# New places in the engines' orders for the Mamba tiles of a four-layer convolution network

## The chip, the cores and the metric

The kernel runs on one core of one Trainium2 chip. The time is that of one execution on the device in microseconds (us); less is better. Three runs of the kernel before gave 7575.1, 7577.68 and 7587.97 us, median 7577.68. A further execution was taken by the profiler: 7595.04 us, with a span of 7593.2 us between its first and last instruction.

## What is computed

The input x is (2, 128, 128, 128) in float32: two images, 128 channels, 128 rows, 128 columns. Four layers follow each other. Layers 0 and 2 are Mamba layers, each with its own weights; layer 1 is a density gate over windows of 8 x 8; layer 3 is a residual block of two 3x3 convolutions with signs as weights. The change touches the Mamba layers alone. At every pixel the 128 channels of a 3x3 convolution are read as a sequence of 8 tokens of 16 features:

```python
seq = conv3x3(x).reshape(B * H * W, 8, 16)
xi, z = split(seq @ in_proj_w.T)                    # 32 each
xc = silu(causal_conv1d(xi) + conv1d_b)
dt, Bm, Cm = split(xc @ x_proj_w.T)                 # 1, 16, 16
dt = softplus(dt @ dt_proj_w.T + dt_proj_b)
dA, dBx = exp(dt * A), dt * Bm * xc                 # 32 x 16 states
h = dA * h + dBx;  y = sum(h * Cm)                  # token after token
out = ((y + D * xc) * silu(z)) @ out_proj_w.T       # 8 x 16 = 128 channels
x = x + silu(group_norm(out))
```

The scan over 8 tokens with 32 x 16 = 512 states a pixel is most of the work.

## The kernel before

A tile (`k` in the code) is 4 image rows, 512 pixels. There are 32 tiles an image, 64 a Mamba layer, 128 in all. All of this is `_mamba` (line 289 on); line numbers are those of the profile.

The work of one tile. `band` loads 8 rows with a border, for two tiles (L191). `conv` is nine matmuls on TensorE (L323) and a copy by ScalarE; `turn` transposes four blocks (L339) and copies; `project` makes xc and z (L350, copies L352 and L354), `silu` L357. `step` makes dt (L364, L365), `softplus` L368. `inout` makes B and C (L400, copy L407), `product` their product on GpSimd (L412), `own` the share of each token's own input (L420, copy L421); `scaled` is u = dt * xc on GpSimd (L374), `own_u` two GpSimd operations (L425, L427) with a scaling by ScalarE between them (L426). `store` writes u and B, C to DRAM in ten small DMAs (L382, L389); `load` reads them back for one token, replicated over the state partitions, in four DMAs: `ur` (L435, L436) and `bcr` (L439, L440). `inject` multiplies the two on GpSimd (L445, 128x2048). `decay` is eight small matmuls (L454) and two exponentials (L463), one for each half of the states; `token` does, for each half, the product with the old state (L472), with C (L473) and the sum of the new state (L477, not for the last token) on VectorE. `gather` sums over the states (L492), onto what `through` put into the same bank (L483); `gate` multiplies with z (L505), `out` is the last matmul (L512, copy L520), `spread` the statistics (L523), `keep` the DMA to y (L527).

Buffers that matter: three `ur`, five `bcr`, four `h`; three PSUM buffers for the decays, of which every decay takes two; one PSUM bank ("one") for all small products and the convolution; one bank ("ys") for the sums and the output. Token 7 of a tile is its last, and token 1 of the next tile comes right behind it; token 0 is the inject of token 0.

The order of every engine is written out by hand. Each step has a place in tokens, relative to its tile's start; a tile is SPAN = 7 tokens long. All steps of all tiles are sorted by `k * SPAN + place` and issued in that order, and each engine works through its own part of the list strictly in order, as data and buffers permit. Thus in the steady state the places of three to four tiles interleave: while tile k is scanned, k+1 is stored and loaded, k+2 is convolved and projected. The first tiles of a layer have an order of their own (`early`), which the change leaves. `token` has fixed places: token t, half jp, at t - 1 + jp / 2. All places are constants:

```python
put(k, REP_AT + t, decay, t)
put(k, t - 1 + jp / 2, token, t, jp)
put(k, SUM_AT + t, gather, t)
```

In the built instruction stream the DMAs of SP carry eight completion semaphores in turn: each waits until the one eight before it has landed, beside its own data and buffers.

Of the kernel before, what the change touches and what calls it, by code (L numbers as in the profile page):

```python
# [266 lines left out]

SPAN = NT - 1
BAND_AT = -22.0
CONV_AT = (-12.75, -12.7, -11.6, -11.5, -11.35, -11.25, -11.2, -11.05, -10.85)  # L270
TURN_AT = -10.5
IN_AT = (-10.0, -9.75, -9.65, -9.05)
SILU_AT = -8.52
BC_AT = (-8.25, -7.45)
DT_AT = (-7.85, -6.7)
SOFTPLUS_AT = -5.62
PROD_AT = -6.85
OWN_AT = (-6.3, -5.8)
U_AT, OWN_U_AT = -5.0, -4.3
STORE_AT = -4.15  # L280
LOAD_AT, INJECT_AT = -3.7, -1.8
REP_AT = -1.2
SUM_AT = 0.35
D_AT = (1.25, 4.2)
V_AT = (3.79, 7.39)
OUT_AT, STATS_AT, KEEP_AT = 7.9, 12.5, 13.85


def _mamba(tc, src, w, con, dst, scratch, stats, H):
# [264 lines left out]
    def put(k, at, f, *args):  # L554
        at = early.get((k, f, *args), k * SPAN + at)
        todo.append((at, len(todo), f, (k, *args)))


    for k in range(len(src) * ntile):
        if k * ROWS % BAND == 0:  # L560
            put(k, BAND_AT, band)
        for tap in range(9):
            put(k, CONV_AT[tap], conv, tap)
        put(k, TURN_AT, turn)
        for n in range(4):
            put(k, IN_AT[n], project, *divmod(n, 2))
        for name in ("xc", "zs"):
            put(k, SILU_AT, silu, name)
        for i in range(2):
            put(k, BC_AT[i], inout, i)  # L570
        for g in range(2):
            put(k, DT_AT[g], step, g)
        put(k, SOFTPLUS_AT, softplus)
        put(k, PROD_AT, product)
        put(k, U_AT, scaled)
        for g in range(2):
            put(k, OWN_AT[g], own, g)
        put(k, OWN_U_AT, own_u)
        put(k, STORE_AT, store)
        for t in range(NT - 1):  # L580
            put(k, LOAD_AT + t, load, t)
            put(k, INJECT_AT + t, inject, t)
        for t in range(1, NT):
            put(k, REP_AT + t, decay, t)
            for jp in range(2):
                put(k, t - 1 + jp / 2, token, t, jp)
            put(k, SUM_AT + t, gather, t)
        for g in range(2):
            put(k, D_AT[g], through, g)
            put(k, V_AT[g], gate, g)  # L590
        put(k, OUT_AT, out)
# [509 lines left out]
```

## Time and profile before

| | |
|---|---|
| median of 3 runs | 7577.68 us (7575.1 to 7587.97) |
| profiled execution | 7595.04 us, span 7593.2 us |
| first Mamba layer, first L472 of tile 0 to that of tile 63 | 68.4 to 3261.2 us |
| second Mamba layer | 3656.9 to 6863.9 us |
| L445 on GpSimd (inject) | 896 times, 4059.2 us, 4537 ns each |
| L472, L473, L477 on VectorE (token) | 1792, 1792, 1536 times, 1223, 1225 and 1214 ns each |
| L463 on ScalarE (exponential of decay) | 1792 times, 1007 ns each |
| DMA issued for `ur` and `bcr` | 896 each, 896 and 448 KB, 11.6 and 11.8 us to landing |
| DMA, mean over the span | 233 GB/s; 250 GB/s in the Mamba layers |

The page gives each engine's busy time, then the span in 40 slices with a digit for the tenths that an engine was busy, then groups of instructions by line with mean durations. The waits say who stood idle for whom: us in total, how often, the longest. A wait for several semaphores is put down to the one that came last. In the timeline each row is a run of equal instructions on one engine, with the idle time before it and what ended it. SPq is the queue from which SP issues DMAs.

### The profile page before, as it was taken

The page shows a single profiled execution, that of the slowest core. Times are in us where ns is not written, and L with a number is a line of the kernel's source. Part 1 is how long each engine was busy: PE and PEld are TensorE (multiplying, and loading weights), DVE is VectorE, ACT ScalarE, POOL GpSimd, SP SyncE. Part 2 cuts the span into 40 slices and gives each one's busy share as a digit, 9 for nine tenths or more (in the row PEclk, how much of TensorE's full clock was granted, in tenths as well). Part 3 has the DMA queues.
Part 4 walks back from the last instruction along what each step waited for, and adds up shares of the span by engine and source line. Part 5 has one row for each costly group of instructions (what it writes and reads, how often), then busy time and mean ns, then how long its engine had stood idle before and what let it go on. Part 6 is the DMA issues. An engine that isn't in the chain of part 4 may idle for free.

```text
span 7593.2 us, 89536 instructions
## 1 busy us (share of the span) xinstructions
PE 6291.6 (83%) x30416; PEld 2339.8 (31%) x30416; DVE 7026.3 (93%) x7082; ACT 4279.0 (56%) x4877; POOL 5538.6 (73%) x1815
## 2 busy tenths in 40 slices
PE   7888888888888888867888888888888888887994
PEld 2222222222222222234222222222222222224773
DVE  6999999999999999968699999999999999998986
ACT  5566656666656666545566656665666566562222
POOL 5778777877787788743687787878777877785641
PEclk8999999999999999977899999999999999997997
DMA  7999999999999999954899999999999999996604
GB/s 207 247 248 250 252 245 251 252 253 249 247 252 255 248 250 253 251 183 173 211 256 245 248 244 248 251 253 246 248 252 248 251 248 246 247 256 184 194 7 172
DMA packets 573737, 1769.79 MB, mean 233 GB/s; under 512 B 85568, under 2 KB 239712, under 8 KB 458208
## 3 DMA queue, kind: packets, MB, share of 16 engines
q1 hardware_dynamic: 568672, 1747.28, 88.1%
q10 hardware_dynamic: 4608, 16.78, 0.6%
q8 instruction: 242, 3.96, 0.2%
q14 instruction: 215, 1.76, 0.1%
HBM read 1552.83 MB, written 210.89 MB: 232 GB/s over the span
## 4 chain that ended last, share of the span: by engine, by line
DVE 39%; DMA 30%; PE 14%; issue 6%; POOL 5%; ACT 4%; SPq 2%; POOLq 0%; DVEq 0%; ACTq 0%
DMA bcr<-sb 23%; DVE set L472 12%; DVE h L477 10%; DVE r L473 10%; DMA ur<-su 4%; PE m L910 4%; POOL h L445 3%; PE set L454 2%; PE one L350 2%; ACT set L463 2%; PE ys L492 1%; PE ys L483 1%; DVE v L505 1%; PE one L400 1%; DVE comb L901 1%
## 5 line engine op out<-in xcount | busy, mean ns | idle before, releaser
L445 POOL TENSOR_TENSOR h<-ur,bcr 128x2048 f32<-128x2048 f32 x896 | 4059.2, 4537 | 1331.9 <-DMA bcr<-sb 1098.7
L472 DVE TENSOR_TENSOR set<-set,h 128x1024 f32<-128x1024 f32 x1792 | 2192.5, 1223 | 257.4 <-ACT set L463 153.8
L473 DVE TENSOR_TENSOR r<-set,bcr 128x1024 f32<-128x1024 f32 x1792 | 2194.4, 1225 | 61.4
L463 ACT ACTIVATE set<-set 128x1024 f32<-128x1024 f32 x1792 | 1743.7, 1007 | 790.0 <-PE set L454 776.4
L477 DVE TENSOR_TENSOR h<-set,h 128x1024 f32<-128x1024 f32 x1536 | 1865.4, 1214 | 43.7 <-POOL h L445 43.1
L454 PE MATMUL set<-dt,rep 32*128 32x512 f32 x7168 | 1385.9, 676 | 97.8 <-DVE h L477 93.5
L492 PE MATMUL ys<-r,ct 128*32 128x512 f32 x7168 | 1160.1, 634 | 33.0 <-DVE r L473 32.6
L323 PE MATMUL one<-band,conv 128*128 128x512 f32 x2304 | 1083.5, 606 | 22.6 <-DMA band<-in_x_dram 12.3
L400 PE MATMUL one<-xc,keep 128*64 128x512 f32 x1008 | 314.8, 707 | 470.3 <-ACT xc L357 355.8
L454 PEld LDWEIGHTS set<-dt,rep 32*128 32x128 f32 x7168 | 403.1, 193 | 977.0 <-issue 478.0
L323 PEld LDWEIGHTS one<-band,conv 128*128 128x128 f32 x2304 | 407.7, 190 | 669.1 <-issue 597.1
L910 PE MATMUL m<-comb,u 128*128 128x256 f32 x2304 | 510.2, 382 | 63.0 <-DVE comb L903 45.3
L483 PE MATMUL ys<-t,ct 128*128 128x512 f32 x512 | 324.5, 720 | 252.1 <-DVE v L505 250.5
L910 PEld LDWEIGHTS m<-comb,u 128*128 128x128 f32 x2304 | 437.5, 191 | 135.4 <-issue 72.0
L492 PEld LDWEIGHTS ys<-r,ct 128*32 128x32 f32 x7168 | 181.2, 111 | 911.3 <-issue 756.9
L352 ACT ACTIVATE xc<-one,keep 128x512 f32<-128x512 f32 x252 | 173.3, 688 | 509.7 <-PE one L350 504.8
L420 PE MATMUL one<-prod,ct 128*128 128x512 f32 x504 | 284.7, 648 | 148.4 <-POOL prod L412 126.7
L374 POOL TENSOR_TENSOR u<-dt,xc 128x1024 f32<-128x1024 f32 x128 | 302.6, 2364 | 78.1 <-ACT dt L368 77.8
L350 PE MATMUL one<-y,w_in 128*128 128x512 f32 x504 | 340.7, 765 | 1.7 <-ACT xc L352 1.7
L421 ACT COPY t<-one 128x512 f32<-128x512 f32 x252 | 147.7, 586 | 326.9 <-PE one L420 326.9
L463 ACT ACT_TABLE_LOAD x254 | 325.9, 1283 | 4.5
L427 POOL TENSOR_TENSOR t<-t,xc 128x1024 f32<-128x1024 f32 x128 | 302.1, 2360 | 10.0
(166 smaller groups left out, 6116.2 us busy)
## 6 DMA issues: line engine op xcount, KB each, us to landing
ur<-su SPq DMA_DIRECT2D x896, 896.0 KB, 11.6
bcr<-sb SPq DMA_DIRECT2D x896, 448.0 KB, 11.8
ur<-su SPq DMA_DIRECT2D x896, 128.0 KB, 11.2
su<-u SPq DMA_DIRECT2D x1024, 64.0 KB, 3.2
sb<-bc SPq DMA_DIRECT2D x256, 224.0 KB, 2.7
bcr<-sb SPq DMA_DIRECT2D x896, 64.0 KB, 11.1
y<-o SPq DMA_DIRECT2D x128, 256.0 KB, 9.2
band<-in_x_dram SPq DMA_DIRECT2D x28, 640.0 KB, 11.0
```

The source lines that it names most:

```text
L323: nc.tensor.matmul(py.rearrange("p (r w) -> p r w", r=ROWS), lhsT=w["conv"][:, tap, :], rhs=xb[:, r + kh : r + kh + ROWS, kw : kw + P], st ...
L350: nc.tensor.matmul(p, lhsT=w[("in", "z")[i]][:, g, :], rhs=s["y"], start=True, stop=True)
L400: nc.tensor.matmul(p[g * NQ * DS : (g + 1) * NQ * DS, :], lhsT=w[("xb", "xcm")[i]], rhs=s["xc"][:, g, :], start=True, stop=True,)
L445: nc.gpsimd.tensor_tensor(b, s["ur", t], s["bc", t][:, 0].unsqueeze(1).to_broadcast([P, NJ, NS]), ALU.mult)
L454: nc.tensor.matmul(a[j // 2][:, j % 2, :], lhsT=w["rep"][r, q, :], rhs=s["dt"][r, g, :], start=True, stop=True, tile_position=(r.start, 0),)
L463: nc.scalar.activation(x, x, AF.Exp)
L472: nc.vector.tensor_tensor(pt, pt, s["h", t - 1][:, js, :], ALU.mult)
L473: nc.vector.tensor_tensor(s["r", t][:, js, :], pt, s["bc", t - 1][:, 1].unsqueeze(1).to_broadcast([P, 2, NS]), ALU.mult)
L477: nc.vector.tensor_tensor(s["h", t][:, js, :], pt, s["h", t][:, js, :], ALU.add)
L483: nc.tensor.matmul(s["ys", g], lhsT=con["ident"], rhs=s["t1"][:, g, :], start=True, stop=False)
L492: nc.tensor.matmul(s["ys", g][a : a + NQ * DJ, :], lhsT=red[:, q, :], rhs=r[:, j, :], start=False, stop=(q == NQ - 1), tile_position=(0, a),)
L910: nc.tensor.matmul(m[:, n // 2, n % 2], lhsT=u[:, i, kw, :], rhs=v[:, i, :, kw : kw + P], start=(kw == 0), stop=(kw == 2),)
```

## The change

Only the table of places is changed. No instruction is added or taken away, no buffer changes its size, and no operation its engine.

```diff
 BAND_AT = -22.0
-CONV_AT = (-12.75, -12.7, -11.6, -11.5, -11.35, -11.25, -11.2, -11.05, -10.85)
-TURN_AT = -10.5
-IN_AT = (-10.0, -9.75, -9.65, -9.05)
-SILU_AT = -8.52
-BC_AT = (-8.25, -7.45)
-DT_AT = (-7.85, -6.7)
-SOFTPLUS_AT = -5.62
-PROD_AT = -6.85
-OWN_AT = (-6.3, -5.8)
-U_AT, OWN_U_AT = -5.0, -4.3
-STORE_AT = -4.15
-LOAD_AT, INJECT_AT = -3.7, -1.8
-REP_AT = -1.2
-SUM_AT = 0.35
-D_AT = (1.25, 4.2)
-V_AT = (3.79, 7.39)
-OUT_AT, STATS_AT, KEEP_AT = 7.9, 12.5, 13.85
+CONV_AT = (-13.2, -12.65, -12.35, -12.1, -11.8, -11.35, -11.3, -11.25, -11.0)
+TURN_AT = -10.9
+IN_AT = (-10.75, -9.2, -10.2, -9.35)
+SILU_AT = -8.87
+BC_AT = (-8.45, -8.05)
+DT_AT = (-8.0, -7.1)
+SOFTPLUS_AT = -6.02
+PROD_AT = -7.75
+OWN_AT = (-7.1, -6.5)
+U_AT, OWN_U_AT = -5.4, -3.15
+STORE_AT = -5.2
+LOAD_AT, INJECT_AT = -4.3, -1.55
+REP_AT = -1.25
+SUM_AT = 0.0
+D_AT = (0.95, 3.85)
+V_AT = (3.29, 7.44)
+OUT_AT, STATS_AT, KEEP_AT = 7.8, 8.0, 12.3
```

Only the order within one engine counts. Over one period (token 1 of tile k to token 1 of tile k+1; +1 and +2 mark steps of the tiles ahead, -1 of the tile behind) the orders become, before and after:

```
VectorE before  1.0 gate1(-1) 1.1 2.0 2.1 3.0 3.1 4.0 4.1 gate0 5.0 5.1 6.0 stats(-1) 6.1 7.0 7.1
VectorE after   1.0 gate1(-1) 1.1 stats(-1) 2.0 2.1 3.0 3.1 4.0 gate0 4.1 5.0 5.1 6.0 6.1 7.0 7.1
GpSimd before   product(+1) inject2 inject3 scaled(+1) inject4 own_u(+1) inject5 inject6 inject0(+1) inject1(+1)
GpSimd after    inject2 inject3 scaled(+1) inject4 inject5 own_u(+1) inject6 inject0(+1) product(+2) inject1(+1)
SP before       load4 load5 load6 store(+1) load0(+1) load1(+1) load2(+1) band(+4) load3(+1) keep(-1)
SP after        load5 load6 store(+1) load0(+1) load1(+1) load2(+1) keep(-1) load3(+1) band(+4) load4(+1)
TensorE before  step1(+1) gather7(-1) own0(+1) decay2 out(-1) own1(+1) through0 conv0 conv1 gather1 decay3
                gather2 conv2-5 decay4 conv6-8 gather3 turn decay5 project00 through1 project01 gather4 project10
                decay6 project11 gather5 inout0 decay7 step0 gather6 inout1 decay1(+1)
TensorE after   gather7(-1) own1(+1) decay2 out(-1) conv0 through0 gather1 conv1 conv2 decay3
                conv3 gather2 conv4-6 decay4 conv7 gather3 conv8 turn project00 decay5 project10 through1 gather4
                project11 decay6 project01 gather5 inout0 decay7 inout1 gather6 step0 decay1(+1) step1 own0
```

(project, conv, turn, inout and step without a mark belong to tile k+2, in the last row step1 and own0 too. ScalarE follows TensorE's order with its copies and exponentials; its SiLUs stay between the exponentials of tokens 6 and 7, its softplus between those of 2 and 3, and the scaling of own_u goes from before the exponentials of token 4 to behind those of token 5.)

## The prediction

> **What bounds the kernel now.** I read the page's first two parts, then who waited for whom on VectorE, then the waits of the stretch 300 to 3300 us (first Mamba layer, all tiles alike), then the timeline of single tiles.
>
> ```profile
> PE 6291.6 (83%) x30416; PEld 2339.8 (31%) x30416; DVE 7026.3 (93%) x7082; ACT 4279.0 (56%) x4877; POOL 5538.6 (73%) x1815
> ...
> DMA  7999999999999999954899999999999999996604
> GB/s 207 247 248 250 252 245 251 252 253 249 247 252 255 248 250 253 251 183 173 211 256 245 248 244 248 251 253 246 248 252 248 251 248 246 247 256 184 194 7 172
> ```
>
> Two candidates stand side by side: VectorE (93%) and the DMA engines, whose digit is 9 through both Mamba layers at a nearly constant 250 GB/s.
>
> VectorE first. In the timeline L472 is followed by L473 after 1.26 us, L473 by L477 after 1.14, L477 by the next L472 after 1.13: 3.53 us for half a token. A tile is 12 such halves (42.36), two halves of token 7 without L477 (2 x 2.40), two L505 (2 x 0.60) and one L523 (0.60): 48.9 us. The fastest tiles are 48.94 us apart, so that is VectorE's floor. The mean distance of tiles is 50.45 us in the first Mamba layer and 50.72 in the second; over 128 tiles the excess is 233 us. What it consists of:
>
> ```profile
> DVE set L472 <- ACT set L463: 153.8, 177, 8.9
> DVE set L472 <- POOL h L445: 97.8, 2, 52.1
> DVE h L477 <- POOL h L445: 43.1, 42, 3.6
> ```
>
> Most is waiting for an exponential. (The 97.8 us are two waits, the layers' starts.) By place, averaged over tiles: 0.65 us before token 6, 0.46 before token 7, 0.25 before token 2, 0.17 before token 3, 0.1 before the next token 1. One wait before token 6:
>
> ```profile
> 3075.13 1.53 PE L483 MATMUL ys<-t,ct 128*128 128x512 f32 x2 [1.95 <-DVE v L505]
> ...
> 3078.40 0.69 ACT L352 ACTIVATE xc<-one,keep 128x512 f32<-128x512 f32 x1 [4.50 <-PE one L350]
> ...
> 3081.91 1.93 ACT L463 ACTIVATE set<-set 128x1024 f32<-128x1024 f32 x2 [0.48 <-PE set L454]
> ...
> 3082.95 1.23 DVE L472 TENSOR_TENSOR set<-set,h 128x1024 f32<-128x1024 f32 x1 [0.82 <-ACT set L463]
> ```
>
> TensorE stands 1.95 us at L483 (`through`) because L505 (`gate`) is late in VectorE's order; everything behind it, the decay matmul L454 too, comes late, and VectorE loses 0.82 us. The wait before token 7 follows: two table loads, two SiLUs and a copy lie between the exponentials of tokens 6 and 7.
>
> Now the load loop.
>
> ```profile
> POOL h L445 <- DMA bcr<-sb: 497.4, 188, 7.1
> ...
> SPq L435 <- DMA ur<-su: 370.9, 164, 4.6
> SPq L382 <- DMA ur<-su: 320.3, 155, 4.5
> ...
> SPq L435 <- POOL h L445: 101.8, 146, 5.1
> ...
> SPq L439 <- DVE r L473: 57.4, 67, 5.4
> ```
>
> SP waits mainly for DMAs to land and for L445 to free a `ur` buffer, hardly for VectorE. In the built order each DMA of SP waits for the one eight before it, two tokens' loads. I compared each bcr issue (L439) with the L473 that frees its buffer: the median issue comes 3.9 us after the release, and in only 25 of 124 tiles does any bcr issue go at the moment of release. So in four tiles of five the loop of SP, DMA and L445 runs at its own pace. From tile 4 to 20 it took 50.79 us a tile, from 84 to 120 50.65, none of it set by VectorE; VectorE's stalls fit into what it leaves. Only from tile 40 to 60 did the loop run ahead: 50.11 against 50.34 for VectorE. A tile moves 7 x 1536 KiB of replicated loads plus 1536 KiB of stores, bands and output, 12.58 MB; at the 250 GB/s of the page 50.3 us. The loop is what bounds.
>
> [...]
>
> **The change, part by part.** No instruction is added or removed; four table loads a tile remain. One frame for all: T6 is the start of token 6, and so on.
>
> *gate 0 half a token earlier (L505), through 1 behind project (1,0).* Gate 0 now needs gather 3, which TensorE ends about 0.1 us after T4, 3.4 us before the gate's place: no new wait. L483 then finds its bank free, and the 1.95 us go. TensorE has between the decays of tokens 5 and 6 project, through, gather, project: 4 x 1.06 = 4.2 us, in 5.8 us (from the second decay half of token 5 to the release of the buffer for that of token 6, both set by L477). Exponential 6 is then bound by that release: L477 ends 3.61 us after T5 (1.26 + 1.14 + 1.21), and where TensorE stood ready the second exponential ended 2.24 us after it (3070.94 to 3073.18); so 5.85 us after T5, 1.21 before T6. The 0.65 us go.
>
> *Token 7.* From the end of exponential 6 to the end of the first half of 7 is 6.96 us in quiet tiles; I take 7.2, as an xc copy (0.69) replaces a zs copy (0.60) and the inout matmul starts a little later. 5.85 + 7.2 = 13.05 after T5, token 7 is due at 14.12: the 0.46 us go, 1.05 us to spare. This holds though L523, which gave this stretch 0.6 us, is moved away.
>
> *step 1, own 0, own 1 around gather 7.* One bank serves all small products, so each waits for the copy before it. From T1: dt copy to 0.7, own 0 to 1.85, gather 7 to 2.9, gate 1 is due at 3.53: no wait. Then own 1 to 4.0, decay 2 to 5.1, out (2.05) to 7.15, o copy (0.59) to 7.8.
>
> *Statistics behind the output.* L523 moves from before token 6.1 to before token 2.0, due at T1 + 7.66; with the semaphore it starts at 7.85: a new wait of 0.2 us a tile. Behind it on VectorE is all of token 2. In the trace of before the o copy ends 0.16 us before token 2 in the median tile: with out one slot later the bounds are 0 and 1.2 us (one more matmul of 1.05 slipping); I take 0.2.
>
> *GpSimd.* product moves ahead of inject 1 and may hold it: it waits for the bc copy at T7 + 0.5 and ends at T7 + 1.85 (0.1 to start, 1.27 busy). Inject 1 starts at T7 + 0.55 in the median tile, so it comes 1.3 us later there; its sum L477 needs it only 2.2 us after its end, and inject 2, which had product ahead of it, starts when it did. In tiles whose data come late GpSimd stands idle before inject 1 anyway (1.7 us in the mean). own_u moves behind inject 5, and its second half now waits for ScalarE's scaling (L426) at T5 + 1.45: inject 6 ends at T5 + 8.45, needed at T5 + 9.46, and inject 0 behind it has 5.4 us of idle time ahead of it. The `ur` buffer that inject 6 frees for load 2 comes 3.8 us later, while load 0 and load 1 (12 us of transfer) are still queued, with 1.6 us to spare. Cost nil with these covers; without them 1.3 and 2 us a tile. L426 itself no longer stands waiting for L374 ahead of an exponential.
>
> *SP.* The loads' numbers say 0.6 token sooner, but on SP the order is load 4, 5, 6, store, load 0, 1, 2, 3 as before. Only keep (one y DMA) goes from behind load 3 to before it, and the band DMA from before load 3 to behind it. Buffers and lanes decide when a load goes, so nothing starts sooner; the same bytes go through the same queue. The gap around the store, where small DMAs follow the last load (13 us from load 6's bcr issue to load 0), has the same order. Cost nil; a band load in another place can shift at most its 2.6 us (655 KB at 250 GB/s) every other tile, and gives it back.
>
> **Sum.** VectorE's own chain falls from about 50.1 us a tile (floor plus 1.1 at tokens 6 and 7) to 49.1. But a tile needs what the load loop needs, and that is untouched. The gain is left where the loop ran ahead and VectorE held it: 25 of 124 tiles, 26 of all 128, each by 0.23 us (50.34 - 50.11, tiles 40 to 60) to 0.6 (if the loop there ran at 49.75, still slower than its best pair of tiles, 49.5). I take 0.4: 26 x 0.4 = 10 us. The profiled execution took 7595.04 us around a span of 7593.2; it would be 7585. Its 17 us over the median of 7577.68 I take as that run's own; on the median: 7567.
>
> **Rivals.** *The loop has room (faster).* If DMA follows a faster VectorE, [...] tiles come down to 49.5, the best pairs of tiles now: (50.6 - 49.5) x 124 = 136 us, less what starts cost; 7460. For it: tiles 40 to 60. Against it: tiles 4 to 20 and 84 to 120, where nothing but itself held the loop at 50.7.
>
> *GpSimd held by ScalarE (slower).* product ahead of inject 1 and own_u ahead of inject 6 bind the load loop to ScalarE's order. If the bc copy comes later than T7 + 1.2, L477 of token 1 waits; if the scaling comes later than T5 + 2.4, load 2 misses its turn and the DMA engines run dry. Price 0.4 us a tile (a third of the 1.3), 51 us: 7628. For it: L445 is in the loop, and both margins are about 1 us. Against: GpSimd's 8 us of idle time a tile.
>
> **How the numbers follow.** About 0.2% (15 us) can be told from no change. Loop-bound as now: 0.52, 7535 to 7600; of it 0.17 faster by over 0.2%, 0.27 within, 0.08 slower. Room in the loop: 0.23, 7430 to 7535, all faster but 0.01. GpSimd held: 0.25, 7595 to 7680; 0.20 slower, 0.05 within. Together faster 0.39, same 0.33, slower 0.28. The range 7475 to 7635 leaves out the far end of each rival, 0.1 and 0.1.
>
> **What would show it.** Right: waits of L472 for L463 fall from 154 us to under 50, L523 appears as waiting for ScalarE, waits of L477 for L445 grow from 43 us to over 100, tile distance and GB/s stay near 50.5 and 250. Wrong: the GB/s row at 255 or more (loop had room), or L445 idle behind product or before L427 (slower rival).

## The result and the profile after

The changed kernel takes 7669.53 us (median of 4 runs, 7661.73 to 7673.01) against 7577.75 (4 runs, 7575.1 to 7587.97): ratio 1.0109, 95% interval 1.0095 to 1.0124. It is slower by about 1.1%. The forecast was 7567. The profiled execution took 7671.14 us, with a span of 7669.3: 76 us more than that of before.

From here on T7 is the start of token 7 of a tile (its first L472), T1 that of token 1 of the next tile, and so on; the distance of tiles is from the first L472 of one to that of the next.

First the page of after: the busy time of TensorE and VectorE, the clock that TensorE was granted, and the DMA rows.

```profile
PE 6565.2 (86%) x30416; PEld 2380.3 (31%) x30416; DVE 7031.7 (92%) x7082; ACT 4283.6 (56%) x4877; POOL 5533.3 (72%) x1815
...
PEclk8999999999999999968899999999999999997997
DMA  7999999999999999964799999999999999996604
GB/s 208 247 246 247 248 245 245 247 247 246 244 249 246 246 245 245 249 194 172 201 251 248 247 246 248 246 248 244 248 246 244 248 246 248 245 246 187 201 7 170
```

VectorE has the same work (7031.7 us), TensorE 274 us more with the same 30416 matmuls: the matmuls themselves got longer. The DMA rate fell from about 250 to 246. In the page's chain of work that ended last the DMAs' share falls from 30% to 7%, and TensorE's rises from 14% to 36%. Then VectorE's waits (us in total, times, longest):

```profile
DVE set L472 <- ACT set L463: 196.3, 124, 12.4
...
DVE stats L523 <- ACT o L520: 62.2, 126, 2.1
```

The waits for the exponential, which were to fall from 153.8 us to under 50, rose; they are 124, about one in every tile, and no longer before tokens 6 and 7. And SP's waits over the whole program:

```profile
SPq L435 <- POOL h L445: 1348.0, 507, 8.0
SPq L435 <- DMA ur<-su: 554.9, 301, 4.8
```

Before, the same two rows were:

```profile
SPq L435 <- DMA ur<-su: 805.9, 374, 4.6
...
SPq L435 <- POOL h L445: 218.5, 317, 5.1
```

Now the loads stand ready and wait for L445 to free a buffer, which it does at the pace of the tokens. The load loop no longer sets the pace.

What does is seen in one tile, T7 = 1651.75. These are rows of the timeline: start, duration, operation, and the idle time before it.

```profile
1646.72 1.08 PE L400 MATMUL one<-xc,keep 128*64 128x512 f32 x4 [1.97 <-ACT xc L357]
...
1647.73 2.79 PE L454 MATMUL set<-dt,rep 32*128 32x512 f32 x8
...
1649.75 1.93 ACT L463 ACTIVATE set<-set 128x1024 f32<-128x1024 f32 x2
...
1650.46 1.98 PE L400 MATMUL one<-xc,keep 128*64 128x512 f32 x4
...
1651.75 1.22 DVE L472 TENSOR_TENSOR set<-set,h 128x1024 f32<-128x1024 f32 x1
...
1652.36 1.94 PE L492 MATMUL ys<-r,ct 128*32 128x512 f32 x8
...
1654.23 1.61 PE L364 MATMUL one<-xc,w_dt 128*128 128x512 f32 x2
...
1655.77 1.14 PE L454 MATMUL set<-dt,rep 32*128 32x512 f32 x8
...
1656.94 1.93 ACT L463 ACTIVATE set<-set 128x1024 f32<-128x1024 f32 x2 [0.38 <-PE set L454]
...
1658.06 1.23 DVE L472 TENSOR_TENSOR set<-set,h 128x1024 f32<-128x1024 f32 x1 [1.42 <-ACT set L463]
```

TensorE waits 1.97 us for SiLU before the first `inout`. Token 7 is on time. But the same groups of matmuls that take 1.08 us (L400), 1.14 (L454) and 1.13 (L364) elsewhere take 1.98, 2.79 and 1.61 between the first `inout` and the decay of token 1, so that token 1 starts 6.31 us after T7 instead of 4.80. The table by stretches shows why. Its columns are busy time and count of each engine, then the granted clock, DMA share and GB/s; the first three stretches belong to this tile, the next three to the following one.

```profile
1641.60:1648.40 6.80, 4.83 (x22) 1.18 (x20) 6.73 (x7) 5.53 (x6) 6.80 (x2) 1.00 0.95 246
1648.50:1655.20 6.70, 6.70 (x19) 1.45 (x18) 6.63 (x6) 3.75 (x4) 4.02 (x4) 0.50 1.01 275
1655.30:1662.10 6.80, 5.16 (x23) 1.36 (x22) 5.22 (x6) 3.79 (x5) 6.80 (x2) 1.00 1.04 240
1692.80:1699.60 6.80, 4.83 (x22) 1.18 (x20) 6.73 (x7) 5.53 (x6) 6.80 (x2) 1.00 1.02 242
1699.70:1706.40 6.70, 6.70 (x19) 1.46 (x18) 6.63 (x6) 3.75 (x4) 3.95 (x3) 0.50 1.02 264
1706.50:1713.30 6.80, 5.16 (x23) 1.36 (x22) 5.22 (x6) 3.79 (x5) 6.80 (x2) 1.00 1.04 255
```

TensorE runs at half its clock for 6.8 us, right there, and 51.2 us later it does so again, with the same busy times of TensorE, VectorE and ScalarE to the hundredth. The clock records of the trace say it for all tiles: half clock from 1648.42 to 1655.25, that is 6.827 us or twice 3.413, then full clock for 44.373 us, or thirteen times 3.413, and so on. (A window here is one such step of 3.413 us: in before and after every record of the clock is a whole number of them, but for the last, where the trace ends.) In 105 of 112 tiles compared (4 to 60 of each Mamba layer), the distance to the next one lies within 0.03 us of 51.20. Before, the distances lay between 48.9 and 54.7 us, 50.46 and 50.72 in the mean of the two layers, and the half clock came mostly as single windows of 3.413 us in changing places, 4.78 us a tile. The SiLU wait of TensorE was there before too, and longer (2.83 us at 3036.18), here with the clock at 1.00 behind it; a row of the timeline of before and the stretch around it:

```profile
3036.18 1.08 PE L400 MATMUL one<-xc,keep 128*64 128x512 f32 x4 [2.83 <-ACT xc L357]
...
3036.00:3041.00 5.00, 4.64 (x22) 1.09 (x22) 4.97 (x6) 4.74 (x6) 3.40 (x4) 1.00 1.02 256
```

The rest of the tile's loss follows from it. The small products behind decay 1 are late, and with them `out`:

```profile
1665.84 0.58 ACT L520 COPY o<-po 128x512 f32<-128x512 f32 x1
...
1666.46 0.69 DVE L523 BATCH_NORM_STATS2 stats<-o 128x6 f32<-128x512 f32 x1 [0.48 <-ACT o L520]
```

By place, in the median tile: 1.50 us before token 1 and 0.75 between token 1 and token 2, 0.55 of it before L523; with the floor of 48.94 they make 51.19. L477 waits 7.1 us in the whole program.

### The profile page after: what moved, and what is told of

It is laid out like the page before. It is cut to its first block, busy times and chain, and to the rows that moved or that the text cites. A ratio compares the mean times of both kernels' runs of the same rounds, so it can differ in the third digit from the quotient of the medians.

```text
span 7669.3 us, 89600 instructions
## 1 busy us (share of the span) xinstructions
PE 6565.2 (86%) x30416; PEld 2380.3 (31%) x30416; DVE 7031.7 (92%) x7082; ACT 4283.6 (56%) x4877; POOL 5533.3 (72%) x1815
## 4 chain that ended last, share of the span: by engine, by line
DVE 41%; PE 36%; issue 8%; ACT 7%; DMA 7%; SPq 1%; POOL 1%; DVEq 0%; POOLq 0%; ACTq 0%
DVE set L472 12%; DVE h L477 12%; DVE r L473 11%; PE set L454 10%; PE ys L492 5%; PE one L400 5%; DMA bcr<-sb 4%; PE m L910 3%; PE one L420 3%; PE po L512 3%; PE one L364 3%; ACT xc L357 2%; ACT set L463 2%; PE one L350 2%; DVE v L505 1%
## 5 line engine op out<-in xcount | busy, mean ns | idle before, releaser
L445 POOL TENSOR_TENSOR h<-ur,bcr 128x2048 f32<-128x2048 f32 x896 | 4051.6, 4535 | 363.5 <-DMA bcr<-sb 291.3
L472 DVE TENSOR_TENSOR set<-set,h 128x1024 f32<-128x1024 f32 x1792 | 2191.8, 1223 | 294.8 <-ACT set L463 196.3
L477 DVE TENSOR_TENSOR h<-set,h 128x1024 f32<-128x1024 f32 x1536 | 1865.7, 1215 | 7.1 <-POOL h L445 7.1
L454 PE MATMUL set<-dt,rep 32*128 32x512 f32 x7168 | 1567.8, 690 | 148.4 <-DVE h L477 148.4
L323 PE MATMUL one<-band,conv 128*128 128x512 f32 x2304 | 1183.1, 623 | 21.1 <-DMA band<-in_x_dram 12.2
L492 PE MATMUL ys<-r,ct 128*32 128x512 f32 x7168 | 1174.5, 678 | 4.4 <-DVE r L473 4.4
L454 PEld LDWEIGHTS set<-dt,rep 32*128 32x128 f32 x7168 | 467.8, 193 | 1140.3 <-issue 474.7
L427 POOL TENSOR_TENSOR t<-t,xc 128x1024 f32<-128x1024 f32 x128 | 301.0, 2352 | 710.4 <-ACT xc L426 603.8
L323 PEld LDWEIGHTS one<-band,conv 128*128 128x128 f32 x2304 | 377.9, 189 | 724.1 <-issue 723.7
L400 PE MATMUL one<-xc,keep 128*64 128x512 f32 x1008 | 386.6, 857 | 251.9 <-ACT xc L357 250.5
L492 PEld LDWEIGHTS ys<-r,ct 128*32 128x32 f32 x7168 | 199.3, 113 | 844.3 <-issue 794.0
L412 POOL TENSOR_TENSOR prod<-bc 128x512 f32<-128x512 f32 x128 | 163.0, 1273 | 310.5 <-ACT bc L407 309.7
L365 ACT ACTIVATE dt<-one,keep 128x512 f32<-128x512 f32 x252 | 173.7, 689 | 355.5 <-PE one L364 355.5
L350 PE MATMUL one<-y,w_in 128*128 128x512 f32 x504 | 285.1, 648 | 85.9 <-ACT y L341 83.7
L364 PE MATMUL one<-xc,w_dt 128*128 128x512 f32 x504 | 346.8, 771 | 3.5 <-ACT bc L407 2.0
```

The lines of the kernel that those rows point to most:

```text
L323: nc.tensor.matmul(py.rearrange("p (r w) -> p r w", r=ROWS), lhsT=w["conv"][:, tap, :], rhs=xb[:, r + kh : r + kh + ROWS, kw : kw + P], st ...
L364: nc.tensor.matmul(p, lhsT=w["dt"], rhs=s["xc"][:, g, :], start=True, stop=True)
L400: nc.tensor.matmul(p[g * NQ * DS : (g + 1) * NQ * DS, :], lhsT=w[("xb", "xcm")[i]], rhs=s["xc"][:, g, :], start=True, stop=True,)
L445: nc.gpsimd.tensor_tensor(b, s["ur", t], s["bc", t][:, 0].unsqueeze(1).to_broadcast([P, NJ, NS]), ALU.mult)
L454: nc.tensor.matmul(a[j // 2][:, j % 2, :], lhsT=w["rep"][r, q, :], rhs=s["dt"][r, g, :], start=True, stop=True, tile_position=(r.start, 0),)
L472: nc.vector.tensor_tensor(pt, pt, s["h", t - 1][:, js, :], ALU.mult)
```

## The experiments

My theory after the trace: TensorE's clock. A rival: the new order of the small products in itself (step 0 behind inout 1 ahead of decay 1), at any clock. A second: the statistics in their new place. A third question was what the load loop still limits. Each ratio below is to the kernel before on the same chip, whose median there was 7599 to 7606 us, so ratios and not microseconds are to be compared. The x, y and z runs ran on three chips, and after itself was not run again beside them: a difference between two rows carries the intervals of both. "Half" is the time at half clock for each tile (tiles 2 to 62), "distance" the mean distance of tiles in the two Mamba layers (tiles 4 to 60).

| run | ratio (95%) | half, us | distance, us |
|---|---|---|---|
| before | 1 | 4.78 | 50.46, 50.72 |
| after | 1.0109 (1.0095 to 1.0124) | 6.83 | 51.20, 51.20 |
| x1_warm_after | 0.9977 (0.9965 to 0.9988) | 1.85 | 50.53, 50.28 |
| x2_stats_back | 0.9982 (0.9970 to 0.9993) | 4.89 | 50.45, 50.47 |
| x3_small_back | 1.0188 (1.0161 to 1.0214) | 5.94 | 51.69, 51.70 |
| x4_warm_before | 1.0005 (0.9989 to 1.0020) | 4.07 | 50.48, 50.94 |
| y1_stats_behind_2 | 0.9967 (0.9955 to 0.9980) | 5.18 | 50.21, 50.41 |
| y2_warm_stats_back | 0.9974 (0.9961 to 0.9987) | 2.30 | 50.41, 50.61 |
| y3_more_bytes_before | 1.0089 (1.0065 to 1.0114) | 5.57 | 50.79, 51.16 |
| y4_more_bytes_after | 1.0106 (1.0088 to 1.0124) | 6.60 | 51.20, 51.32 |
| z1_more_dve | 1.0101 (1.0078 to 1.0125) | 7.59 | 51.19, 51.24 |
| z2_gate_back | 0.9977 (0.9968 to 0.9987) | 3.13 | 50.33, 50.53 |
| z3_warm_stats_behind_2 | 0.9975 (0.9962 to 0.9989) | 1.85 | 50.56, 50.56 |
| z4_same_elsewhere | 1.0083 (1.0063 to 1.0102) | 5.52 | 51.03, 51.15 |

**x1_warm_after: fill the gap.** The changed kernel with two matmuls more in front of inout 0, where TensorE stands; inout overwrites what they write.

```diff
     def inout(k, i):
...
         p = one(k)
+        for _ in range(2 * (i == 0)):
+            nc.tensor.matmul(p, lhsT=w["in"][:, 0, :], rhs=s["y"], start=True, stop=True)
```

> The changed kernel with two more matmuls a tile (128x128 weights, 512 columns, result overwritten) in front of inout 0, in the 1.97 us in which TensorE waits for the SiLU of xc. Clock theory (TensorE's granted clock falls to a half for 6.83 us a tile behind that gap, and the products up to decay 1 take twice as long): the half clock goes, to under 2 us a tile, the wait before token 1 falls from 1.5 us a tile to under 0.3, and the kernel takes 7530 to 7580 us. Order theory (the chain of small products through one bank is too long at any clock): at least 7660 us, since two matmuls are added, and the wait before token 1 stays at 1.5 us.

Measured: 7590.26 us (by the ratio 7560 where before takes 7577.75). More work for TensorE, and 1.3% less time than after. T7 to T1 is 4.80 us in the median tile of this kernel, and of its 56 spells of half clock 1 begins between 6 and 2 us before T7. Its waits (lines from L402 on are two higher here):

```profile
DVE h L479 <- POOL h L447: 122.9, 81, 4.1
...
DVE stats L525 <- ACT o L522: 42.7, 45, 3.6
...
DVE set L474 <- ACT set L465: 30.7, 42, 10.3
```

The waits for the exponential fell from 196.3 to 30.7 us, and those for inject (L445, here L447) came in their place: 122.9, of which 86.3 where inject had itself just waited for its `bcr` load. The half clock behind the gap is what cost the time.

**z4_same_elsewhere: the same two matmuls, not in the gap.** In front of the transposes of `turn`.

```diff
     def turn(k):
...
         p = one(k)
+        for _ in range(2):
+            nc.tensor.matmul(p, lhsT=con["ident"], rhs=s["yc"], start=True, stop=True)
```

> The changed kernel with two more matmuls of the same size where TensorE has no long gap: in front of the transposes of turn, between the decays of tokens 4 and 5. If it was the filled gap before inout 0 that helped, nothing is gained here: tiles stay at 51.20 us or above, half clock at 6.8 us a tile, ratio 1.009 to 1.02. If any further work on TensorE keeps its clock up: ratio 0.997 to 1.003, as with the gap filled.

Measured: 1.0083, 0.0007 under what was expected, the interval reaching into it; half clock 5.52 us a tile, not 6.8, and the distances a little under 51.20. The time alone settles little, for these matmuls also make a wait that after does not have: 0.60 us a tile before token 5, in 111 of 112 tiles, while the loss before token 1 falls from 1.50 to 0.84 us. So there are more waits for the exponential than in after, 208 against 124:

```profile
DVE set L474 <- ACT set L465: 180.9, 208, 13.4
```

What can be compared is where the half clock falls: 109 of its 111 spells begin 6 to 2 us before T7, as in after, against 1 of 56 in x1. Work in the gap takes the half clock from there; the same work elsewhere does not.

**x4_warm_before: the same in the kernel before.**

> The kernel before with the same two matmuls in front of inout 0 (its gap is 2.8 us). If the load loop binds it as forecast, the time stays within 7560 to 7590 us, though the waits before token 7 fall from 57 us to under 20. If its waits for exponentials bind it, and these come from the half clock, it falls to 7480 to 7540.

Measured: no change. Before, most of the loss stood elsewhere: half clock came mainly where TensorE stood at through 1 (84 of the 149 spells in before begin 22 to 12 us ahead of T7, there 0.45 us in the median after the end of that wait of 1.94 us), and the wait at that place stays. The loss before token 7 fell, as expected (from 0.46 to 0.14 us a tile), but the one before token 3 rose (from 0.17 to 0.40).

**x3_small_back: the old order of the small products.**

```diff
-BC_AT = (-8.45, -8.05)
-DT_AT = (-8.0, -7.1)
-PROD_AT = -7.75
-OWN_AT = (-7.1, -6.5)
+BC_AT = (-8.25, -7.45)
+DT_AT = (-7.85, -6.7)
+PROD_AT = -6.85
+OWN_AT = (-6.3, -6.22)
```

> The changed kernel with inout 1, step 0 and 1, product and own 0 at their old places (own 1 at -6.22, behind decay 2), so that step 0 comes before inout 1 and gather 7 before own 0. Order theory: exponential 1 comes 1.1 to 1.5 us earlier, the wait before token 1 falls under 0.3 us and gate 1 waits no more: 7500 to 7560 us. Clock theory: the gap before inout 0 is as it was, a half-clock stretch lies behind it, and the stretch from there to decay 1 holds the same matmuls: 7620 to 7680 us.

Measured: 7744.14 us, outside what either theory gave. The rival has fallen: with the old order it is not faster. But my theory didn't give 1.0188 either. The median tile loses 1.75 us before token 1 and 0.74 behind it (48.94 + 2.49 = 51.43, the median distance is 51.44), with single windows of half clock that begin about 9 and about 2 us before T7. The loss before token 1 has the size of the half clock: at a granted 0.5, one window of 3.413 us costs a chain that keeps TensorE busy 1.71 us, and two windows 3.41 (an estimate from the clock records). Tiles with one window just before T7 lose 1.75 in the median; the 16 of 112 tiles with two in a row there lose 3.40 and take 53.09 us, which lifts the mean to 51.7. What this order would take at full clock wasn't tried.

**x2_stats_back and y1_stats_behind_2: the statistics elsewhere.** In x2 L523 and `keep` go back to their old places (12.5, 13.85). In y1 L523 stays in the stretch but comes half a token later, behind the first half of token 2, where o has been copied:

```diff
-OUT_AT, STATS_AT, KEEP_AT = 7.8, 8.0, 12.3
+OUT_AT, STATS_AT, KEEP_AT = 7.8, 8.5, 12.3
```

> The changed kernel with the statistics and the output DMA at their old places (12.5 and 13.85). Added waits counted one by one: the 0.55 us a tile of L523 go, 7600 us. Clock theory: the distance of tiles (51.20 us, 15 clock windows of 3.413 us) is set by where the half-clock stretch ends, so what is saved at L523 comes back before token 1; 7655 to 7672 us.

> The changed kernel with the statistics half a token further back (8.5: between the halves of token 2), so that the o copy is there 3 us before L523 and nothing waits for it, while the stretch from token 6 to token 7 stays without it. If the wait of L523 is what costs: as with the statistics at their old place, 7570 to 7600 us. If it is the 0.6 us that L523 gave VectorE between tokens 6 and 7, where TensorE runs at half clock: the wait before token 1 stays (1.4 us a tile or more) and the kernel takes 7630 to 7680 us.

Measured: 0.9982 and 0.9967. The clock theory had x2 stay at 51.20; that was a miss. y1 came out where its expectation put it if the wait of L523 is what costs (7582 us, within 7570 to 7600). Only a wait of 0.55 us goes, yet 0.75 to 1 us a tile is won and the fixed period is gone: the trace of x2 has no distance within 0.03 us of 51.20, that of y1 one. So the wait of L523 doesn't only add its own time: without it the chain no longer reaches 51.20, the half clock wanders from tile to tile as it did before, and falls where it hurts only now and then. The longest distance that the chain itself gave in after is 51.24 us (its first tiles), so a chain that is 0.55 us shorter falls short of 51.20. VectorE's largest wait in x2 is then the one for inject:

```profile
DVE h L477 <- POOL h L445: 142.2, 123, 3.7
```

y1 has the lowest ratio found, ahead of both kernels, though its interval overlaps those of x1, y2, z2 and z3.

**z2_gate_back: undo gate 0 alone.** The step that the forecast counted as the gain, taken back:

```diff
-V_AT = (3.29, 7.44)
+V_AT = (3.79, 7.44)
```

> The changed kernel with gate 0 alone at its old place (3.79, behind token 4.1), so that TensorE stands at through 1 for some 2 us as before. By the forecast's own count this brings back the wait before token 6, 0.65 us a tile and 83 us: ratio 1.018 to 1.025. Clock theory: the gap at through 1 draws a half-clock window to token 5, as in the kernel before, and the stretch before token 1 is then at half clock in part of the tiles only: the lock at 51.20 us breaks, ratio 0.997 to 1.006.

Measured: 0.9977, 1.3% faster than after, as the clock theory had it. TensorE stands at `through` again, and VectorE's wait for the exponential is small all the same:

```profile
PE ys L483 <- DVE v L505: 176.2, 128, 2.5
```

```profile
DVE h L477 <- POOL h L445: 109.3, 93, 4.0
...
DVE set L472 <- ACT set L463: 45.8, 25, 11.0
```

The half clock still comes in front of T7 (82 of 86 spells), but as a single window in 62 of them: 3.13 us a tile instead of 6.83. Taking the stall at `through` away is thus one condition of the slowdown, not a gain, in company with the other edits.

**z1_more_dve and y4_more_bytes_after: more work in the changed kernel.** z1 adds a second `bn_stats` of 0.6 us a tile to VectorE's order, y4 a further DMA of 256 KB a tile to DRAM, in `keep`. If a chain of VectorE or the loads set the period, they would add to it.

```diff
+    def more(k):
+        again = tmp.tile([P, 6], F32, tag="again", name="again")
+        nc.vector.bn_stats(again, live[k]["o"])
...
+        put(k, 10.6, more)
```

```diff
     def keep(k):
...
+        extra = scratch.tile([P, NS], F32, tag="extra", name="extra")
+        nc.sync.dma_start(out=extra, in_=live[k]["o"])
```

> The changed kernel with the statistics computed a second time, into a spare tile, behind token 4 (0.6 us more on VectorE in each tile). If each tile's 51.20 us are a lock (the wait before token 1 lasts until TensorE's half-clock stretch has ended, and that ends on a grid of 3.413 us), the new work comes out of the 1.5 us wait: tiles stay 51.20 us apart, ratio to before 1.008 to 1.013. If the waits follow VectorE's own chain, they stay and the work is added: 0.6 us x 126 = 76 us, ratio 1.019 to 1.023.

> The changed kernel with the same further DMA. Its tiles are 51.20 us apart, 0.7 above what the load loop needs by the forecast; with 1.05 us more the loop comes to 51.5, so 0.3 to 0.5 us a tile: ratio to before 1.014 to 1.019 (1.011 without it). If the DMA engines have more room: still 1.010 to 1.012.

Measured: 1.0101 and 1.0106, both as after itself. Of z1:

```profile
DVE set L472 <- ACT set L463: 133.4, 103, 11.6
...
DVE stats L523 <- ACT o L520: 55.8, 119, 2.5
```

The two waits sum to 189.2 us instead of 258.5: 69 us, or 0.55 of the added 0.6 a tile. Work put in comes out of the waiting, so no chain of VectorE with fixed waits sets the pace. But z1 does not keep the pattern of after: its distance is 51.2 only in the mean (2 of 120 tiles lie within 0.03 us of 51.20, the medians are 51.29 and 51.31), it has 7.59 us of half clock a tile, and 40 of its 120 spells last three or four windows. In y4 the pattern stays: 110 of its 120 spells are double windows, 78 of 120 tiles lie within 0.03 us, and the median distances are 51.20 and 51.195. The added DMA tells that the loads have room there; it lies outside the chain that ends at token 1.

**y3_more_bytes_before: the same DMA in the kernel before.** It tells how far the loop bound that kernel. 256 KB at 250 GB/s are 1.05 us.

> The kernel before with one more DMA of 256 KB a tile (the output tile written a second time, to scratch). If the load loop binds it: 262 KB at 250 GB/s are 1.05 us a tile, 134 us in all, ratio to before 1.015 to 1.02. If VectorE's chain binds it and the DMA engines have room: under 1.004.

Measured: 1.0089, and 0.33 and 0.44 us a tile in the two layers, between the two expectations. The loop bound the kernel before only in part. (Its waits for the exponential grew as well, from 153.8 to 183.8 us, so not all of the 0.33 and 0.44 need be the loop.)

**y2_warm_stats_back and z3_warm_stats_behind_2: two cures at once** (x1 with x2, x1 with y1).

> The changed kernel with both remedies: two more matmuls in the gap before inout 0, and the statistics at their old place. If the two add up (each took some 80 us off the changed kernel): 7500 to 7520 us. If behind VectorE's chain the load loop binds at 50.5 us a tile, as forecast: 7560 to 7595 us, like either alone, with L477 waiting for L445 over 100 us in all.

> The changed kernel with the statistics between the halves of token 2 and two more matmuls in the gap before inout 0. If the half clock still costs the 0.7 us before token 1 that are left with the statistics there: 50.2 less 0.5, ratio to before 0.988 to 0.993. If the load loop takes over: ratio 0.994 to 0.999, with L477 waiting for L445 over 100 us.

Measured: 0.9974 and 0.9975, no better than one alone. In z3:

```profile
DVE h L479 <- POOL h L447: 179.7, 122, 4.0
...
DVE set L474 <- ACT set L465: 30.6, 36, 9.2
```

With the clock mended VectorE waits for inject instead, in nearly every tile. Of the 179.7 us, 112.5 come where inject had just waited for its `bcr` load, and 34.4 where it ran straight behind own_u or product; in y2 it is 80.2 and 57.6 of 167.0. So at 50.4 to 50.6 us a tile the load loop binds in the main, as the forecast had it, and GpSimd's new order, the forecast's slower rival, takes a smaller part. No run took these two apart.

**A count over all traces.** I laid the grid of 3.413 us windows over all fourteen traces (the clock records of one trace lie on one grid to 0.01 us) and summed, for each window in which the clock was full, the matmul work in it, counted 0.1 us ahead of the grid. The price of a full 128x128 matmul with 512 columns is the timeline's step at full clock: in the trace of z2 a run of six L323 takes 2.84 us, one of four 1.99, so about 0.43 each (0.427 was taken); the others are estimated from it by their share of rows, columns and length (0.213 for L400, 0.107 for L454, L492 and L512).

| | |
|---|---|
| windows counted | 21,776, of which 1526 are followed by half clock |
| best single limit | 1.24 us of work |
| on the wrong side of it | 207 (1%); in before 8 of 1550, in after 2 of 1484 |
| work in the windows ahead of half clock, after | 1.07 to 1.16 us (5% to 95%) |
| work in the windows that kept the clock, after | 99% at 1.45 us or more |

The limit and the 0.1 us are fitted to these traces, not measured apart, and how a matmul at a window's edge is divided between two windows moves the work ahead of half clock by about 0.1 us (a second count gave 1.19 to 1.22 in after, the same limit, and 216 windows on the wrong side). Time that TensorE was busy, in place of work, separates far worse: its best limit leaves over 600 windows on the wrong side. So the changed kernel runs close to the edge: its window around inout 0 is short of the limit by 0.2 us of matmuls at most, in every tile.

## Why the prediction was wrong

**What held.** *gate 0, through 1:* L483 waits for nothing, and the 0.65 us before token 6 are gone. *Token 7:* it waits for nothing; its exponential comes 1.0 us ahead of need, as worked out (1.05). *SP and the loads:* nothing starts sooner, no bytes change. *GpSimd:* L427 does stand behind ScalarE's scaling (710.4 us idle, 603.8 of it for L426), which the prediction had named as a sign of the slower rival, but L477 waits only 7.1 us; that cover was there, and that rival is not the cause though its side was right. (It shows only with the clock mended, as in z3.)

**What failed, first: "step 1, own 0, own 1 around gather 7 ... no wait" and the unsaid step before it.** The sum of the change took all matmuls between inout 0 and decay 1 at the durations of the profile before, 1.06 to 1.14 us a group, and found token 1 in time. They took 1.61 to 2.79 us. The bc copy that product waits for was worked out for T7 + 0.5; it ends at T7 + 1.31, the dt copy behind it at T7 + 4.81, and token 1 starts 1.50 us late. The durations of a group of matmuls were taken as constants; in these traces they follow the granted clock (L454 1.14 us at 1.00, 2.79 where most of it falls at 0.50), and the clock falls behind a window of 3.413 us with little matmul work in it (under the fitted limit of 1.24 us above). The clock records of before and after have 0.5 or 1.00 and nothing between, in steps of 3.413 us on one grid. The sum of the change had no clock in it, though before spends 4.78 us a tile at half clock.

**Second: removing a stall was counted as a gain alone.** z2 shows that with the stall of L483 put back the slowdown is gone. With it removed, and the statistics behind the output, one gap is left, at inout 0; the chain from there to token 2 with half clock in it makes the tile 48.94 + 1.50 + 0.75 = 51.19 us, and fifteen windows are 51.20. So the next tile meets the windows in the same phase, its gap makes the clock fall again, and so through both layers. That it is held there, and not met by chance, the trace of after shows where one tile comes late. In the second layer (tiles counted through, 64 to 127) tile 96 lost 0.73 us at token 2:

| tile | half clock begins before T7, us | T7 to T1, us | T7 to the next T7, us |
|---|---|---|---|
| 95 | 3.34 | 6.30 | 51.94 |
| 96 | 4.08 | 5.93 | 50.83 |
| 97 | 3.71 | 6.12 | 51.02 |
| 98 | 3.52 | 6.21 | 51.11 |
| 99 | 3.43 | 6.26 | 51.15 |
| 100 | 3.38 | 6.28 | 51.18 |
| 103 | 3.34 | 6.30 | 51.20 |

A late tile has less of the half clock left behind T7, by as much as it is late, and at half clock it loses half as much less: tile 96 is 0.74 us off the 3.34 of tile 95 and takes 0.37 less from T7 to T1. So every tile halves the deviation (0.74, 0.37, 0.18, 0.09 and 0.04 us in tiles 96 to 100), and the phase returns to where a tile takes fifteen windows. The first layer came to the same phase from the other side: 3.13 us in its tile 1, 3.33 from tile 8 on. And in x2, y1 and z2 one small edit frees the tiles from it.

**Third: "a new wait of 0.2 us" at L523.** It was 0.55 us in the median tile (62.2 us in 126 times in the whole program, 0.49), inside its bounds of 0 and 1.2. Its size was off because out came late by the slow products; its weight was off because it tips the period.

**Fourth: "the loop is what bounds."** Right in part. y3 shows under half of an added load in the kernel before (0.33 and 0.44 of 1.05 us); z3 and y2 show the loop binding in the main at 50.4 to 50.6 us once the clock is mended, where I had 50.5. But in the changed kernel it has room: SP waits mainly for L445 (1348.0 us), less than before for DMAs (554.9 against 805.9), and y4's 1.05 us vanish in it. With the chain at 51.20 the loop could not matter. The rival "loop has room" (7460) is not borne out by any version; the best, y1, gains 0.3%.

By the sum: the forecast took 0.08 us a tile off (10 us in 128). Measured are 0.74 and 0.48 us more in the two layers, 46 and 30 us over 62 tiles each, which is the 76 us of the spans. (The forecast's 233 us of excess over VectorE's floor holds for the whole layers with their first tiles; the two mean distances given beside it make 211 us over 128 tiles.)

**What stays open.** Why the half clock lasts two windows each time in after (120 of 120 spells, tiles 2 to 62) and mostly one in before (149 spells, 19 of them longer): the work in the first slow window doesn't tell them apart. In z1 and z4 the place does: of the spells that begin in the 7 us before T7, those more than about 4.4 us ahead of it last one window (22 and 25), the later ones two or more (44 and 77), and in after nearly all begin 3.3 us ahead. The reason stays open. So does what x3 would take at full clock, and how much of the wait for inject in the mended kernels is GpSimd's order.

## What to carry to other kernels

Price matmuls only with the clock that the stretch will have (here 1.06 to 1.14 us a group at 1.00, and 1.61 to 2.79 in and at the edges of the stretch at 0.50): look at the clock column of short stretches of the trace, and before a change removes or moves a stall of TensorE, ask which gap is then left and whether a serial chain follows it. Here a period that repeats to the hundredth of a microsecond (51.20), and comes back after a tile that was 0.73 us late, pointed to something outside the program's own waits: the grid of the clock. Two idle-time matmuls ahead of the chain (1.3% here) or half a token's distance for one waiting instruction cured it; both together gave no more, since the next limit, in the main the loads, stood a good 1% away.

## What the runs showed of the hardware that I had not expected

- A gap far under a window can be enough. In after 1.97 us did it, in every tile, where the matmuls around the gap filled only about 1.1 to 1.2 of the window's 3.41 us. (In before, a gap of 2.83 us left the clock at 1.00 at 3036.18.) In all fourteen traces a fitted limit of about 1.24 us of matmul work in a window, a good third, separates the two cases with 1% on the wrong side.
- A busy TensorE is not a clock-keeping TensorE: in the slow stretch it is busy 6.70 of 6.70 us, at 0.50.
- The program's period can settle on a multiple of the clock's window: 51.20 us, fifteen times 3.413, in 105 of 112 tiles. A tile that came 0.73 us late was back within 0.1 us after three more. With 0.6 us more of VectorE's work or 256 KB more of DMA a tile the time stayed the same (1.0101 and 1.0106 beside 1.0109).
